# Another order of the seven products of a fast 2x2 block multiplication, and another interleaving of the steps, in a graph-network kernel

## The chip, the core and the metric

The kernel runs on one core of a Trainium2 chip. A core has five engines with a queue each: TensorE (PE in the profile; PEld is its loading of weights) multiplies matrices, VectorE (DVE), ScalarE (ACT) and GpSimd (POOL) work on elements, and SyncE (SP) issues the transfers between the main memory and the on-chip memory SBUF. TensorE writes its products into PSUM, eight banks of 128 x 512 fp32, from where VectorE and ScalarE read them. Each engine takes its instructions strictly in the order in which they were written; an instruction that waits for another engine holds up everything behind it in its own queue.

The metric is the time of one execution in microseconds (us) on the device.

## The reference

Everything is fp32. For 64 graphs of 256 nodes and 512 features, with a dense adjacency matrix each:

```
# layer 0
h = relu(adj @ (x @ W1) + b1)
h = relu(adj @ (h @ W2) + b2)
h = adj @ (h @ W3) + b3
x = layernorm(x + h)
# layer 1
q, k = split(x @ Wqk);  v = x @ Wv
agg = adj @ (k * mask)
w = (q * agg).sum(-1) * mask / sqrt(512)
x = layernorm(x + softmax(w)[:, None] * v)
```

The softmax runs over the nodes of a graph, one weight for each node.

## The kernel before

**Tiling.** Two graphs make a pair, and there are 32 pairs. A product of two matrices, cut into 2 x 2 blocks, is made with seven block products instead of eight (Strassen's scheme in Winograd's form): sums of blocks are made ahead of them (`a_sums`, `b_steps`, `t_sums`, `adj_sums`), and sums of the products behind them. This is what `seven()` (L110) writes out: `mm(n, bank, first)` issues the matmuls of product n into a PSUM bank, with `first=False` adding to what the bank holds. Three banks are used: x collects products 1, 6, 5, 3; v collects 7 and 4; y holds 2. The four blocks of the result come out as

- C11 = y + P1 (P1 copied out of x by ScalarE right after product 1, L117);
- U = P1 + P6 is copied out of x after product 6 (L126);
- after product 5 bank x holds U + P5, which ScalarE copies to `q` (L134); C22 = v + q is summed by VectorE (its adds are all in `add`, L65);
- C12 is what x holds after product 3, C21 = v + u after product 4.

With `plus`, three more blocks are added to C11, C22 and C21: GpSimd adds them to the copies of P1, q and u (`padd`, L68). For the order 1, 7, 6, 2, 5, 3, 4 this means: product 3 goes into bank x once ScalarE has copied it to q, and product 4 into bank v once VectorE has read it for C22.

`seven()` is called from three places. `support` (L306) makes x times a weight matrix, four matmuls to a product. `adj_times` (L364) makes adjacency times a matrix, two matmuls to a product; it is used in `back` (layer 0's third aggregation, with x + b3 as `plus`) and for the gather `agg`. `inner` (L543) is one of two levels of the attention: the 2 x 2 scheme is applied twice, seven outer products in the groups "a" (1, 2), "b" (6, 5), "c" (7, 4), "d" (3), each made of seven inner ones, whose order is `STEPS`, "ab" seven times, then "cd" seven times. "c" and "d" have `plus`. The weights of the inner products were summed once (`make_m`), lie in main memory, and are fetched by SP into a ring of seven tiles: each inner step issues the fetch of the tile seven steps on (`fetch`, L230). The first two aggregations (L328) use plain blocks: their four column tiles of 128 features go through ScalarE's relu (L331) into hT, in the order 2, 3, 0, 1; `lower_first` swaps the two halves, so that the sums of the next support can start with the lower half of the features. All weight matrices W1, W2, W3 are held with their rows in that swapped order.

**Stages.** Generators yield after each step: F is the front of pair i (support, aggregation, support, aggregation, support); S the sums for the next pair and x + b3; B the back of pair i-1 (the third aggregation, layer norm, transposition of the result by way of main memory, `via`); G its gather; M its attention, which ends with `results` (the two scores of each graph, L560, on VectorE, and half of v); E finishes pair i-2 (softmax with transposes on TensorE at L383 and L398, scaling of v at L601, layer norm, output). In the last round X and Y finish the two graphs of the last pair.

**What sets the order.** Three strings written out in the code, START for the first round, ORDER for rounds 1 to 31, and END for the last: each letter runs one step of that generator, and `run()` goes through the string (L631). Since every engine takes its instructions as written, these strings and the order inside the steps decide what stands behind what in all five queues.

## Time and profile before

| | |
|---|---|
| runs shown | 2795.99, 2801.28, 2804.63 us; median 2801.28 |
| the profiled execution | 2800.18 us, span 2798.4 us |
| mean granted TensorE clock | 0.994 |
| busy: TensorE, GpSimd, VectorE, ScalarE | 2741.9, 1817.1, 1718.5, 1158.0 us |
| matmul records, first and last start | 12688, 1.4 and 2788.2 us |

An fp32 matmul is recorded as two records, so a product of a support shows as 8 matmul records, one of `adj_times` as 4. The span runs from the first to the last instruction of the program; the profiled execution's own time is a little longer. A line of the timeline names start, duration, engine, line of the kernel, operation, output and inputs, shape and how many instructions were put together; in brackets is how long the engine had been idle, and who ended it. In the waits, "A <- B" means that A's engine stood idle until B was done.

The bias add x + b3 (L68, `x<-x,b3b`) takes 1.49 us on average; the additions of `plus` in `back` (`tmp<-tmp,x`) 1.41; ScalarE's copies out of a bank 0.56 (L117, L126, L134); VectorE's adds from a bank 0.62 to 0.68 (L65). A fetch into the ring lands 3.3 us after its issue in the median, the load of x, 1 MB, 6.6.

### The profile page before, as it was taken

To read this page: it belongs to the slowest core of one execution; us is meant where nothing else is said; L and a number is where in the kernel's file an instruction comes from. 1 tells how busy PE (TensorE), PEld (TensorE's weight loads), DVE (VectorE), ACT (ScalarE), POOL (GpSimd) and SP (SyncE) were. 2 spreads that over 40 slices of the span, in tenths; PEclk is the share of its full clock that TensorE was granted. 3 is DMA by queue.
4 is the path that set the end of the run, shared out by engine and by line. 5 is a ranking of instruction groups with operands and counts; after the bars stand their busy time and mean duration, and the time that the engine had idled before them with its cause. 6 is when DMAs were issued, how large, how long until landed. Compare 5 with 4: busy or idle time off the path is not lost.

```text
span 2798.4 us, 36927 instructions
## 1 busy us (share of the span) xinstructions
PE 2741.9 (98%) x12688; PEld 2370.7 (85%) x12688; DVE 1718.5 (61%) x2898; ACT 1158.0 (41%) x1888; POOL 1817.1 (65%) x1446
## 2 busy tenths in 40 slices
PE   9999999999999999999999999999999999999996
PEld 8888888888888888888888888888888888888875
DVE  4466556666556666556665566665566655666556
ACT  2334344434444334444343444344443434443444
POOL 2667766676766676666667666766666776667664
PEclk9999999999999999999999999999999999999998
DMA  6444554344554344544445543445444455434442
GB/s 216 138 125 145 160 175 133 117 141 150 160 160 135 115 145 146 174 144 129 124 144 160 175 132 112 140 146 172 150 131 125 134 160 175 132 115 145 134 153 96
DMA packets 197752, 403.45 MB, mean 144 GB/s; under 512 B 20160, under 2 KB 57408, under 8 KB 189504
## 3 DMA queue, kind: packets, MB, share of 16 engines
q1 hardware_dynamic: 197568, 401.10, 44.8%
q8 instruction: 103, 1.69, 0.3%
q14 instruction: 81, 0.66, 0.1%
HBM read 328.54 MB, written 72.48 MB: 143 GB/s over the span
## 4 chain that ended last, share of the span: by engine, by line
PE 91%; DMA 3%; POOL 2%; DVE 2%; ACT 1%; issue 1%; SPq 0%; ACTq 0%; DVEq 0%; POOLq 0%
PE ps L306 39%; PE ps L543 22%; PE ps L328 16%; PE ps L364 13%; DMA ring<-mv 3%; POOL tmp L68 2%; DVE r L65 1%; ACT tmp L134 1%; PE ps L248 1%; PE ps L383 0%; PE ps L398 0%; DMA xT<-in_xT 0%; DVE w L97 0%; POOL x L68 0%; POOL T L97 0%
## 5 line engine op out<-in xcount | busy, mean ns | idle before, releaser
L306 PE MATMUL ps<-w_T,S 128*128 128x256 f32 x2304 | 547.7, 381 | 2.4 <-POOL S L289 1.9
L306 PEld LDWEIGHTS ps<-w_T,S 128*128 128x128 f32 x2304 | 432.6, 190 | 61.4 <-POOL S L289 3.1
L65 DVE TENSOR_TENSOR R<-ps,tmp 128x512 f32<-128x512 f32 (+1 forms) x384 | 235.5, 621 | 385.5 <-PE ps L543 327.6
L328 PE MATMUL ps<-aT,sup 128*128 128x256 f32 x2048 | 457.7, 379 | 0.0
L543 PE MATMUL ps<-ring,I 128*128 128x256 f32 x1792 | 425.1, 381 | 13.8 <-DMA ring<-mv 12.1
L328 PEld LDWEIGHTS ps<-aT,sup 128*128 128x128 f32 x2048 | 389.1, 190 | 52.8
L285 POOL TENSOR_TENSOR S<-hT 128x512 f32<-128x512 f32 x64 | 81.9, 1280 | 538.1 <-ACT hT L331 538.1
L543 PEld LDWEIGHTS ps<-ring,I 128*128 128x128 f32 x1792 | 335.1, 190 | 72.6 <-ACT tmp L134 18.4
L134 ACT COPY tmp<-ps 128x512 f32<-128x512 f32 (+1 forms) x288 | 161.0, 559 | 541.9 <-PE ps L306 305.8
L65 DVE TENSOR_TENSOR sup<-ps,tmp 128x512 f32<-128x512 f32 x288 | 196.5, 682 | 244.8 <-PE ps L306 192.2
L543 PE MATMUL ps<-ring,Z 128*128 128x256 f32 x1344 | 322.6, 380 | 0.0
L68 POOL TENSOR_TENSOR tmp<-tmp,R 128x512 f32<-128x512 f32 x192 | 229.4, 1208 | 125.5 <-ACT tmp L134 50.6
L117 ACT COPY tmp<-ps 128x512 f32<-128x512 f32 (+1 forms) x288 | 161.2, 560 | 313.6 <-PE ps L306 133.6
L543 PEld LDWEIGHTS ps<-ring,Z 128*128 128x128 f32 x1344 | 256.1, 191 | 35.0
L126 ACT COPY tmp<-ps 128x512 f32<-128x512 f32 (+1 forms) x288 | 158.6, 562 | 287.9 <-PE ps L306 154.9
L306 PE MATMUL ps<-w,hT 128*128 128x256 f32 x1024 | 241.9, 379 | 0.0
L331 ACT ACTIVATE hT<-ps,b 128x512 f32<-128x512 f32 x256 | 175.6, 686 | 119.8 <-PE ps L328 114.4
L68 POOL TENSOR_TENSOR I<-Z 128x384 f32<-128x384 f32 (+1 forms) x128 | 171.8, 1363 | 77.7 <-ACT Z L521 77.0
L306 PEld LDWEIGHTS ps<-w,hT 128*128 128x128 f32 x1024 | 194.6, 190 | 26.5
L364 PE MATMUL ps<-T,aS 128*128 128x256 f32 x768 | 197.1, 386 | 2.6 <-POOL T L97 2.6
L68 POOL TENSOR_TENSOR tmp<-tmp,x 128x512 f32<-128x512 f32 x96 | 134.3, 1413 | 99.7 <-ACT tmp L134 99.7
L68 POOL TENSOR_TENSOR x<-x,b3b 128x512 f32<-128x512 f32 x128 | 189.4, 1489 | 0.0
(111 smaller groups left out, 4522.9 us busy)
## 6 DMA issues: line engine op xcount, KB each, us to landing
ring<-mv SPq DMA_DIRECT2D x672, 256.0 KB, 3.3
x<-in_xN SPq DMA_DIRECT2D x32, 1024.0 KB, 6.6
out<-v SPq DMA_DIRECT2D x64, 512.0 KB, 2.7
xT<-in_xT SPq DMA_DIRECT2D x31, 1024.0 KB, 4.8
via<-tr SPq DMA_DIRECT2D x31, 1024.0 KB, 4.3
x1T<-via SPq DMA_DIRECT2D x124, 256.0 KB, 4.4
ring<-mv SPq DMA_DIRECT2D x224, 128.0 KB, 2.7
aT<-in_adjT SPq DMA_DIRECT2D x32, 512.0 KB, 3.3
```

Of the source, the lines that this page charges most:

```text
L65: nc.vector.tensor_tensor(o, a, b, op=OP.add)
L68: nc.gpsimd.tensor_tensor(o, a, b, op=op)
L117: nc.scalar.copy(t1, x)
L126: nc.scalar.copy(u, x)
L134: nc.scalar.copy(q, x)
L248: nc.tensor.matmul(pt[:, j * P:(j + 1) * P], lhsT=wq[:, d, f * P:(f + 1) * P], rhs=wk[:, d, j * P:(j + 1) * P], start=(d == 0 and j == 0), ...
L285: eng.tensor_tensor(S[2], blk(0, 0), blk(1, 0), op=sub)
L306: nc.tensor.matmul(ps[:, g], lhsT=src[n][:, c, g], rhs=w[n][:, c], start=(first and g == 0 and c == 0), stop=(g == G - 1 and c == 1), skip ...
L328: nc.tensor.matmul(ps[:, g], lhsT=C[k][c // 2][:, g, (c % 2) * P:(c % 2 + 1) * P], rhs=aT[:, k, g], start=(g == 0 and k == 0), stop=(g == ...
L331: nc.scalar.activation(hT[c // 2][:, c % 2], ps, AF.Relu, bias=b[:, c:c + 1])
L364: nc.tensor.matmul(ps[:, g], lhsT=aS[n][:, g], rhs=mov[n][:, g], start=(first and g == 0), stop=(g == G - 1), skip_group_check=True)
L543: nc.tensor.matmul(ps[:, k], lhsT=left[n](place[o]), rhs=wt[:, k], start=(first and k == 0), stop=(k == len(outer) - 1), skip_group_check= ...
```

## The change

- In `seven()` the order is 1, 7, 6, 2, 5, 4, 3. After product 2, ScalarE copies P7 out of bank v into `t7` (with `plus`, GpSimd adds there to t7 and u). After product 5, VectorE sums C22 from bank x, which holds U + P5, and t7. Product 4 then goes into bank v, and C21 = v + u; product 3 goes last into bank x, and C12 is what it then holds. ScalarE makes as many copies as before. `INNER`, the order in which the ring's weights are stored and fetched, follows.
- The column tiles of the aggregations go in the order 0, 1, 2, 3; `blocks` replaces `lower_first`, and only the input xT and W1 keep the lower half first.
- `results(1)` comes before `results(0)`, and X and Y change places.
- In the last round r lies where xT did, and the transposed x1T is in two tiles, each with its own copies out of PSUM.
- All strings of steps are different. The last full round has a string of its own (the same as ORDER), and whatever it leaves of the attention of pair 30 would be run in END as "N"; the padding that follows a string is named for each round.

```diff
--- before.py
+++ after.py
@@ -111,6 +111,7 @@
 
 
 
+
         x = bank(shape)
         mm(1, x, True)
         t1 = shaped(shape)
@@ -127,28 +128,25 @@
         yield
         y = bank(shape)
         mm(2, y, True)
+        t7 = shaped(shape)
+        nc.scalar.copy(t7, v)
+        if plus is not None:
+            padd(t7, t7, plus[2])
+            padd(u, u, plus[1])
         c11(y, t1)
         yield
         mm(5, x, False)
-        q = shaped(shape)
-        nc.scalar.copy(q, x)
-        if plus is not None:
-            padd(q, q, plus[2])
-        else:
-            c22(v, q)
-        yield
-        mm(3, x, False)
-        if plus is not None:
-            c22(v, q)
-            padd(u, u, plus[1])
-        c12(x)
+        c22(x, t7)
         yield
         mm(4, v, False)
         c21(v, u)
         yield
-
-
-    def load_w(w, n):
+        mm(3, x, False)
+        c12(x)
+        yield
+
+
+    def load_w(w, n, lower=False):
 
 
         q = [tmp().rearrange("p (c f) -> p c f", c=2) if b == 1 else
@@ -156,7 +154,7 @@
         ts = [const.tile([P, 2, HD], FP, name=f"w{n}_{s}") for s in KEYS]
 
         def load(b):
-            k, j = 1 - b // 2, b % 2
+            k, j = (1 - b // 2 if lower else b // 2), b % 2
             nc.sync.dma_start(q[b], w[k * HD:(k + 1) * HD, j * HD:(j + 1) * HD].rearrange("(c p) f -> p c f", p=P))
 
         def begin():
@@ -180,7 +178,7 @@
 
     warm(10)
     wl = {}
-    begin, end = load_w(W1, 1)
+    begin, end = load_w(W1, 1, True)
     xTs = load_xT(0, begin)
     for _ in end():
         pass
@@ -211,7 +209,7 @@
 
 
     OUTER = ((1, 2), (6, 5), (7, 4), (3,))
-    INNER = (1, 7, 6, 2, 5, 3, 4)
+    INNER = (1, 7, 6, 2, 5, 4, 3)
     STEPS = "ab" * 7 + "cd" * 7
     place = {n: k for k, n in enumerate(n for q in OUTER for n in q)}
     w_dram = [dram.tile([P, 7, len(q), HD], FP, name=f"mv_{k}", bufs=1) for k, q in enumerate(OUTER)]
@@ -292,9 +290,9 @@
             eng.tensor_tensor(S[3], blk(0, 1), S[1], op=sub)
         return {1: blk(0, 0), 2: blk(0, 1), 4: blk(1, 1), 5: S[0], 6: S[1], 7: S[2], 3: S[3]}, first, rest, last
 
-    def lower_first(hT):
-
-        return lambda h, k: hT[1 - k][:, :, :, h * P:(h + 1) * P]
+    def blocks(hT, lower=False):
+
+        return lambda h, k: hT[1 - k if lower else k][:, :, :, h * P:(h + 1) * P]
 
     def support(src, w, last=None):
 
@@ -320,8 +318,8 @@
 
 
         hT = [pool.tile([P, 2, G, N], FP, name="hT", tag="act", bufs=2) for _ in range(2)]
-        src, first, rest, last = a_sums(lower_first(hT))
-        for c in (2, 3, 0, 1):
+        src, first, rest, last = a_sums(blocks(hT))
+        for c in range(DC):
             ps = bank()
             for g in range(G):
                 for k in range(NH):
@@ -329,9 +327,9 @@
                                      rhs=aT[:, k, g], start=(g == 0 and k == 0), stop=(g == G - 1 and k == NH - 1),
                                      skip_group_check=True)
             nc.scalar.activation(hT[c // 2][:, c % 2], ps, AF.Relu, bias=b[:, c:c + 1])
+            if c == 1:
+                first()
             if c == 3:
-                first()
-            if c == 1:
                 rest()
             yield
         return src, last
@@ -415,7 +413,7 @@
 
         fs = [lambda: None] * 3
         if i + 1 < NPAIR:
-            put["S"], *fs = a_sums(lower_first(put["xT"]))
+            put["S"], *fs = a_sums(blocks(put["xT"], True))
         for f in fs:
             f()
             yield
@@ -428,7 +426,7 @@
 
     def back(i, C, aS, x, end, put):
         Ts = t_sums(C)
-        r = pool.tile([P, G, NH, D], FP, name="r", bufs=1)
+        r = pool.tile([P, G, NH, D], FP, name="r", tag="xT" if end else "r", bufs=1)
         xb = lambda h, j: x[:, :, h, j * HD:(j + 1) * HD]
         rb = lambda h, j: r[:, :, h, j * HD:(j + 1) * HD]
         st = small.tile([P, NH, G, 6], FP, name="st")
@@ -463,8 +461,8 @@
         xmb = [[xm[:, :, h, j * HD:(j + 1) * HD] for j in range(2)] for h in range(2)]
         if end:
             warm(20)
-            x1T = pool.tile([P, 2, 2, G, N], FP, name="x1T", bufs=1)
-            x1b = lambda h, k: x1T[:, k, :, :, h * P:(h + 1) * P]
+            x1T = [pool.tile([P, 2, G, N], FP, name="x1T", tag="act", bufs=2) for _ in range(2)]
+            x1b = lambda h, k: x1T[k][:, :, :, h * P:(h + 1) * P]
             for h, g in hg:
                 apply(h, g)
             yield
@@ -474,7 +472,8 @@
                 pt = bank((P, 2, 2, P))
                 for c in range(DC):
                     nc.tensor.transpose(pt[:, c // 2, c % 2], r[:, g, h, c * P:(c + 1) * P], ident)
-                (nc.scalar.copy if h else nc.vector.tensor_copy)(x1T[:, :, :, g, h * P:(h + 1) * P], pt)
+                for k in range(2):
+                    (nc.scalar.copy if h else nc.vector.tensor_copy)(x1T[k][:, :, g, h * P:(h + 1) * P], pt[:, k])
         else:
             tr = pool.tile([P, 4, 32, NH, 2, 2, G], FP, name="tr", tag="gt", bufs=1)
             x1T = pool.tile([P, P, NH, 2, 2, G], FP, name="x1T", bufs=1)
@@ -584,10 +583,10 @@
                 C = pool.tile([P, 2, G, 2, HD], FP, name="R", tag="Za", bufs=1)
                 run.update(c=inner(2, C, B), d=inner(3, B[:, :1], B[:, :1]))
             if n == 26:
-                yield from results(0)
+                yield from results(1)
             next(run[k])
             yield
-        yield from results(1)
+        yield from results(0)
 
     def finish(i, prev, gs=range(G)):
 
@@ -621,29 +620,31 @@
 
 
 
-    ORDER = ("FBFEFFEFEBBBBFBBFBFBFBFFBBBFEFBEBGFSGFFGEGFEEGEEFEFFFEMMGGMFMMFMMMMMSMSMMMMMMMMMMFMS"
-             "MMFMMMMMFMMSESMSMSMFMSMSMMMFFSM")
-    START = ("BFFBBFFFBFBBBBFBBFBBBBBBBFBFBBFFBBBBBBBFFBFBBBFBFBBFBBFBBBFFBFBBBBFBBFFBFBBBBBFSBBBB"
-             "SSSBBFSSBSFSBSBSBBBSBSB")
-    END = ("BEEBEEBEEBBBBEBBBBEBEEBBBGGEMMBBMGGMEMGMMGMBMMMGMMMMMMMMMMMMMMMMMMMMMMMMXMMMMMXXMMYX"
-           "XMMMXMYMMMYYXXYXYXXMYYYXYYY")
-
-    def run(order, **gens):
+    ORDER = ("BFEFFFEBFBEFBBBFBBFBBFFFBFBESBEFBBGFFGEFEEGEGFFEFESFFGMMGSFEMGMMFMMMMMMMMMMMMMMMMMFM"
+             "MMMMMSFMMMSSMMSMSSFMFSMFMMEMSMMFM")
+    START = ("FBBFBFFFBBFBBBFBBFBBBBFBFFBBBBBBFBBFBBBBBBBBFFFFBBFBBBBBBFFBBSBFFBFBBSFBBBFFSBBBFSBB"
+             "BBSBFBSBFBSSSSBSBBBSBBB")
+    LAST = ("BFEFFFEBFBEFBBBFBBFBBFFFBFBESBEFBBGFFGEFEEGEGFFEFESFFGMMGSFEMGMMFMMMMMMMMMMMMMMMMMFM"
+            "MMMMMSFMMMSSMMSMSSFMFSMFMMEMSMMFM")
+    END = ("EEBEBEBEEBBBEEEBBBEEBBBBBBGMGMGBGMMBMEMMMMMGGMMMBMMMMGMMMMMMMMMMMMMMMMMMXMXMMMMXMMYM"
+           "XMXXMXMYMYYYXXYYMMXXMYXYYYY")
+
+    def run(order, rest, **gens):
         res = {}
-        for k in order + "FSBGMEXY" * 90:
+        for k in order + rest * 90:
             if k in gens and k not in res:
                 try:
                     next(gens[k])
                 except StopIteration as e:
                     res[k] = e.value
-        assert len(res) == len(gens)
+        assert all(k in res for k in rest if k in gens)
         return res
 
     def later(put, f):
         yield from f(put)
 
     state = prev = None
-    xS, *fs = a_sums(lower_first(xTs))
+    xS, *fs = a_sums(blocks(xTs, True))
     for f in fs:
         f()
     for i in range(NPAIR + 1):
@@ -658,13 +659,17 @@
             for k in "GM":
                 gens[k] = later(done, lambda d, k=k: d[k])
         if prev is not None:
-            gens["E"] = finish(i - 2, prev)
-        if i == NPAIR:
-            for g, k in enumerate("XY"):
+            gens["E"] = later(prev, lambda d, i=i: finish(i - 2, d[0]))
+        if i < NPAIR - 1:
+            res = run(ORDER if i else START, "FSBGME", **gens)
+        elif i < NPAIR:
+            res = run(LAST, "FSBGE", **gens)
+            rest = gens["M"]
+        else:
+            for g, k in enumerate("YX"):
                 gens[k] = later(done, lambda d, g=g: finish(NPAIR - 1, d[g], [g]))
-        order = START if i == 0 else ORDER if i < NPAIR else END
-        res = run(order.replace(" ", ""), **gens)
-        prev = done.get(1)
+            run(END, "NBGMEXY", N=rest, **gens)
+        prev = done if i else None
         if i < NPAIR:
             state = (res["F"], put["aS"], put["x"])
             xTs, xS = put.get("xT"), put.get("S")
```

## The prediction

> **What bounds the kernel now.** I read the page first: busy time of the engines, the slices, the chain that ended last.
>
> ```profile
> span 2798.4 us, 36927 instructions
> PE 2741.9 (98%) x12688; PEld 2370.7 (85%) x12688; DVE 1718.5 (61%) x2898; ACT 1158.0 (41%) x1888; POOL 1817.1 (65%) x1446
> PE   9999999999999999999999999999999999999996
> PE ps L306 39%; PE ps L543 22%; PE ps L328 16%; PE ps L364 13%; DMA ring<-mv 3%; POOL tmp L68 2%; DVE r L65 1%; ACT tmp L134 1%; PE ps L248 1%; PE ps L383 0%; PE ps L398 0%; DMA xT<-in_xT 0%; DVE w L97 0%; POOL x L68 0%; POOL T L97 0%
> ```
>
> TensorE is the bound: 98% busy, 91% of the chain. The number of matmuls does not change, so the change can only win the holes between them, or open new ones. I measured the holes as distances between the starts of successive matmul records, against the 0.2157 us that undisturbed ones keep (8 records in 1.73 us below, which is one product of a support; a product of `back` is 4 records, 0.863 us). All holes together are 81 us of the span. Next the waits, longest first, of which these bear on the change:
>
> ```profile
> POOL tmp L68 <- ACT tmp L134: 150.3, 95, 5.9
> DVE r L65 <- POOL tmp L68: 24.4, 32, 2.1
> PEld ps L364 <- DVE r L65: 18.6, 32, 1.3
> PE ps L543 <- DMA ring<-mv: 12.1, 14, 1.6
> ```
>
> (Who waited for whom: us in total, times, longest.) Only the last two rows are TensorE's. 32 times it waits at L364, once per pair; 14 times for a weight tile of the ring. Third, TensorE's timeline around L364 in one middle pair:
>
> ```profile
> 1025.85 1.03 PE L364 MATMUL ps<-sup,aT 128*128 128x256 f32 x4
> 1026.74 1.13 PE L364 MATMUL ps<-T,aS 128*128 128x256 f32 x4
> 1027.71 1.89 PE L306 MATMUL ps<-w,S 128*128 128x256 f32 x8
> 1029.43 1.03 PE L364 MATMUL ps<-sup,aS 128*128 128x256 f32 x4
> 1030.61 1.13 PE L364 MATMUL ps<-T,aT 128*128 128x256 f32 x4 [0.15 <-DVE r L65]
> 1031.58 1.89 PE L306 MATMUL ps<-w_T,xT 128*128 128x256 f32 x8
> ```
>
> The reader should subtract starts: product 3 of `back` (sup,aS) takes 1.18 us to the next start instead of 0.863, product 4 (T,aT) 0.97. Steady pairs without a ring hole repeat every 84.59 to 84.60 us, of which 0.86 us is holes; 0.20 of these stand at the softmax transposes, the rest in the lines shown.
>
> **The change, part by part.**
>
> *Order of the products in `back`.* Removed is the chain product 5, ACT copy L134, POOL add L68, DVE add into r, product 4: (1.18 - 0.863) + (0.97 - 0.863) = 0.42 us. Removed too is the edge of product 5 (T,aS at 1026.74, after 6): 0.89 + 0.97 - 2 x 0.863 = 0.135 us, since ACT has one copy less to make between 6 and 3. Together 0.557 us in each of 31 pairs: 17.3 us. Product 4 now finds its bank v free, because P7 was copied out two products earlier. The new wait is product 3 on the DVE add that reads bank x. Product 4 (2 matmuls) and a product of a support (4) lie between, 2.6 us; from the end of a product to DVE's start the timeline shows about 0.25 us, the add L65 is 0.68. Queued ahead of it on DVE are four softmax scalings (L601, 4.40 us in this pair), two adds of the next support, a bn_stats and the add for C11; walked through in the new order, they leave the bank's release some 1.6 us early. With every scaling at its largest in the trace, 1.76 us, it would be 1.0 late, 31 us over the run; at their mean, 1.16, it is not late, and I take nothing. Behind that add wait this pair's bn_stats and, through product 3, its layer norm. The two POOL adds (L68, 1.41 us each) and the ACT copy (0.56) move one or two steps ahead in their queues; the 150.3 us that POOL spent waiting for ACT show that POOL had room there.
>
> *Order in the supports and the attention.* In the steady pairs product 3 after an ACT copy cost next to nothing there (other work stood between), so nothing is won. Lost may be two narrow places that I found by counting matmuls (0.4313 us each) in the new order of instructions. (i) Support 3: product 3 stands 7 matmuls, 3.0 us, behind product 5, and waits for a DVE add that is queued behind two scores (L560), the add for C11 (0.68) and half of v (0.67 to 1.14). (ii) The softmax transposes (L383 before, L381 after) come 11 matmuls, 4.75 us, after product 3 of "d", where 19 stood before; between lie DVE adds of 0.69 and 0.41 and two scores. What a score costs is the question:
>
> ```profile
> 1008.63 0.75 DVE L560 SCALAR_TENSOR_TENSOR gt<-R,mask_s,gt 128x512 f32<-128x512 f32 x1
> 1009.31 1.74 DVE L560 SCALAR_TENSOR_TENSOR gt<-R,mask_s,gt 128x512 f32<-128x512 f32 x1
> 1013.69 1.40 DVE L560 SCALAR_TENSOR_TENSOR gt<-R,mask_s,gt 128x512 f32<-128x512 f32 x1
> 1015.02 1.20 DVE L560 SCALAR_TENSOR_TENSOR gt<-R,mask_s,gt 128x512 f32<-128x512 f32 x1
> ```
>
> (Start, us, on VectorE.) The same instruction takes 0.75 us alone and 1.74 beside POOL's `x + b3b`. With two of 1.20 to 1.27, the median and mean, DVE is some 0.5 us early at (i) and 0.2 to 1.0 early at (ii). With two of 1.74 it is about 0.6 late at (i) and, at worst, 1.1 late at (ii): 1.7 us per pair, 51 us over 30 pairs. The other end is nothing, as these places are not waited at before. I take 0.2 us per pair, 6 us: near the lower end, because the four scores above average 1.27. [...]
>
> *The ring.* Its holes average 0.52 us per pair, 15 us in 29 pairs. They fall at the third fetch of an a/b phase, issued on SP's queue just behind the 1 MB load of x (6.6 us to land), 13 matmuls before use. Load, fetches and distance stand the same after; I keep the 15 us (ends: 0, and 1.7 us in every pair, 49). In the c/d phase the fetches now stand 13 to 15 matmuls (5.6 us at least) ahead of use instead of 17 to 19; in one pair of the trace they landed 2.4 to 4.1 us after issue, so I count nothing (upper end, landing like the 6.6 us of x: 1 us per pair, 30). Other SP work (`via`, x1T, out, aT) keeps its place to within a few matmuls; xT is fetched 12 matmuls earlier into a quiet stretch.
>
> *Columns in order 0..3, upper rows first.* First sums wait for two activations as before; distances are the same to a matmul. Nothing; the POOL sums S have 538 us of waiting in front of them as cover.
>
> *Start.* Three supports run back to back there:
>
> ```profile
> 52.96 1.97 PE L306 MATMUL ps<-w,S 128*128 128x256 f32 x8 [0.77 <-ACT tmp L134]
> 73.25 1.97 PE L306 MATMUL ps<-w,S 128*128 128x256 f32 x8 [0.77 <-ACT tmp L134]
> 77.29 3.28 PE L306 MATMUL ps<-w_T,hT 128*128 128x256 f32 x8 [2.08 <-DVE sup L65]
> ```
>
> Each loses about 1.0 us at product 3 (0.92 ahead of it by starts, 0.09 after; the first at 18.05). Product 4's 1.73 us now stands where that hole was, and covers 0.25 + 0.68 of DVE. That wins 3 us. The 2.08 at 77.29 is DVE busy with the sums of the attention's weights and stays, at product 3. Bounds: 0 (the holes move to that queue) and -6 (that wait goes too).
>
> *End.* The last `back` stands alone:
>
> ```profile
> 2734.91 1.13 PE L364 MATMUL ps<-sup,aS 128*128 128x256 f32 x4 [0.73 <-ACT tmp L134]
> 2736.97 1.13 PE L364 MATMUL ps<-T,aT 128*128 128x256 f32 x4 [0.94 <-DVE r L65]
> ```
>
> Both waits go, 1.67 us; about 0.5 comes back at product 3 (0.25 + 0.68 + rest against 0.863), and x1T in two tiles makes 8 copies of half the size from 4, on two engines, some +0.3. With the earlier sums T, the sum is -1.5 (bounds -5, +2: X and Y change places, and each wait in the tail is 2 to 4 us).
>
> **Sum.** The profiled execution took 2800.18 us (span 2798.4), 1.1 under the median of the runs, 2801.28. 2800.2 - 17.3 + 6 - 3 - 1.5 = 2784.4, about 2784.
>
> **Rivals.**
>
> *R1, slower: VectorE late for bank x and for the softmax.* Mechanism (i) and (ii) at the long scores: 2800.2 - 17.3 - 4.5 + 51 = 2829. It decides from 0.557 us per pair on, plus 0.15 for start and end: a second score at 1.74 instead of 1.2 nearly does it at (i). For it: 1.74 is in the trace, and POOL is busy with x + b3b and aS just then. Against: the mean is 1.27, the largest of 128 is 1.77, and a delay at (i) also delays what (ii) stands behind.
>
> *R2, no change: the same places take 0.3 to 0.6 us per pair.* 2800.2 - 21.8 + 9 to 18 = 2787 to 2796; only its upper half is within 0.3%.
>
> *R3, slower: ring fetches.* With 1.73 us less distance, c/d fetches that land late cost up to 1 us per pair: 2778 + 30 = 2808, with a few us of (i) 2815. For it: a third fetch already lands late in 14 pairs. Against: these stand behind x's load, those do not.
>
> *R4, faster still: no new hole.* 2800.2 - 21.8 = 2778. *R5, nothing is won:* were the holes merely taken over by the ring, steady pairs would stay at 2796 or so. Against: where a ring hole occurs, the 0.42 at L364 is there as well, and x's load is released by TensorE's own progress.
>
> **How the numbers follow.** Chances: the forecast 0.45 (own range 2776 to 2792), R4 0.22, R2 and R5 0.17, R1 0.10, R3 0.06. 0.3%, 8.4 us, is about what a measurement of this kernel can tell from no change: faster is under 2793, slower over 2810. R1's lower half and part of R2 fall between: faster 0.69, same 0.17, slower 0.14. For 8 in 10 the range goes from 2774 (R4 with a better start) to 2808 (R3, R1 just past its turn); the far part of R1 is left out.
>
> **What would show it.** Right: pairs without a ring hole repeat every 84.0 to 84.2 us; no row of PEld L362 waiting for DVE r; the pair's starts at L362 0.86 apart; no 0.77 waits at L304 near 50 and 70 us. Wrong: rows of TensorE at L304 waiting for DVE sup, at L381 waiting for DVE gt in most of 32 pairs, at L362 for DVE r; ring waits well over 12 us; DVE's L559 mean far over 1.27.

## The result, and the profile after

The changed kernel takes 2779.19 us (median of 4 runs, 2775.05 to 2780.69); the kernel before, in the same comparison, 2800.02 us. The ratio is 0.9923, with a 95% interval of 0.9904 to 0.9942: 0.8% faster, 4.8 us below the forecast of 2784 and inside its own range. In a second comparison, with more runs, the same two kernels stood at 2790.21 and 2802.65 us, ratio 0.9946 (0.9930 to 0.9962). Why the gain is 21 us in the one and 12 in the other is answered below: it is not the change that differs.

The page of the changed kernel, its span, busy times and chain by line:

```profile
span 2778.9 us, 37024 instructions
PE 2731.4 (98%) x12688; PEld 2377.9 (86%) x12688; DVE 1723.4 (62%) x2900; ACT 1143.7 (41%) x1890; POOL 1795.9 (65%) x1446
PE ps L304 41%; PE ps L542 22%; PE ps L326 16%; PE ps L362 14%; DMA ring<-mv 3%; PE ps L246 1%; DVE v L600 0%; DVE gt L559 0%; PE ps L381 0%; PE ps L396 0%; DMA xT<-in_xT 0%; DVE R L65 0%; POOL S L286 0%; POOL tmp L68 0%; DVE st L607 0%
```

The line numbers have moved by two or so: L304 are the supports (306 before), L362 `adj_times` (364), L542 the attention, L326 the aggregations, L381 the first softmax transposes. The 2% of POOL tmp L68 in the chain is 0% now, and DVE r L65 and ACT tmp L134, 1% each, are no longer named. The same in the waits (us in total, times, longest):

```profile
POOL tmp L68 <- ACT tmp L132: 147.4, 63, 4.4
PE ps L542 <- DMA ring<-mv: 13.1, 13, 1.5
PE ps L381 <- DVE gt L559: 7.7, 3, 3.5
PEld ps L362 <- DVE r L65: 1.8, 1, 1.8
```

PEld waited 32 times for DVE r; one time is left, in the last round. The ring's wait stands as it did. TensorE's timeline around `back` in one pair:

```profile
1022.69 1.03 PE L362 MATMUL ps<-sup,aT 128*128 128x256 f32 x4
1023.55 1.03 PE L362 MATMUL ps<-T,aS 128*128 128x256 f32 x4
1024.41 1.03 PE L362 MATMUL ps<-T,aT 128*128 128x256 f32 x4
1025.28 1.89 PE L304 MATMUL ps<-w,S 128*128 128x256 f32 x8
1027.00 1.03 PE L362 MATMUL ps<-sup,aS 128*128 128x256 f32 x4
1027.87 4.48 PE L326 MATMUL ps<-aT,sup 128*128 128x256 f32 x20
```

Every product of `back` now takes 0.86 to 0.87 us to the next start; in the kernel before it was 0.89, 0.97, 1.18 and 0.97. Product 4 (T,aT) follows product 5 at once, and product 3 (sup,aS) comes last, with a support's product between.

I add up TensorE's holes as in the prediction: the distance between the starts of two successive records, less 0.2157 us, wherever it is over 0.225. The start reaches to the first product with the next pair's xT, the end begins after the last product of a support.

| holes, us | before | after |
|---|---|---|
| start | 10.4 | 7.0 |
| rounds 1 to 31 | 44.7 | 29.4 |
| of these: at the attention's matmuls, nearly all the ring's | 20.2 | 16.9 |
| `back`, product 4 | 13.1 | 0 |
| `back`, product 5 | 4.1 | 0 |
| edges at the softmax transposes | 6.0 | 6.0 |
| support 3, product 3 | 0 | 6.5 |
| all else | 1.2 | 0 |
| end | 25.8 | 24.8 |
| together | 80.9 | 61.2 |

Pairs in which the ring is not late repeat every 84.15 us instead of 84.59. The 0.44 us are 0.56 of `back` less 0.21 at support 3, and 0.10 in the attention, where the old order lost as much to the copy at its inner product 3 (in the kernel before it shows only where the ring is not late; in run 12, where it never is, in all 31 rounds).

The difference, 19.7 us, is close to the 19.5 between the two profiled executions, 2800.18 and 2780.69. The row that is new, 6.5 us at support 3's product 3, is seen where VectorE frees bank x. VectorE in a middle pair:

```profile
1001.48 1.73 DVE L559 SCALAR_TENSOR_TENSOR gt<-R,mask_s,gt 128x512 f32<-128x512 f32 x1
1003.14 1.74 DVE L559 SCALAR_TENSOR_TENSOR gt<-R,mask_s,gt 128x512 f32<-128x512 f32 x1
1004.81 0.68 DVE L65 TENSOR_TENSOR sup<-ps,tmp 128x512 f32<-128x512 f32 x1
1005.42 1.14 DVE L65 TENSOR_TENSOR v<-R 128x512 f32<-128x512 f32 x1
1006.48 0.68 DVE L65 TENSOR_TENSOR sup<-ps,tmp 128x512 f32<-128x512 f32 x1
```

and TensorE at the same time:

```profile
1006.74 0.59 PE L542 MATMUL ps<-ring,I 128*128 128x256 f32 x2
1007.31 1.96 PE L304 MATMUL ps<-w,S 128*128 128x256 f32 x8
1009.11 1.03 PE L362 MATMUL ps<-sup,aT 128*128 128x256 f32 x4
```

C22 is the last of VectorE's lines: it starts at 1006.48 and ends after 1007.1. Product 3 could start at 1006.74 + 0.43 = 1007.17 and starts at 1007.31: 0.14 us, and 0.07 more on its first records. Both scores in front take their full 1.73 and 1.74 us.

In the start, product 3 no longer waits for a copy; two waits of about 2 us are left, the second of them at a product 3, but for VectorE:

```profile
12.44 1.99 PE L304 MATMUL ps<-w_T,S 128*128 128x256 f32 x8 [2.06 <-POOL S L287]
53.38 1.89 PE L304 MATMUL ps<-w,S 128*128 128x256 f32 x8
74.81 1.97 PE L304 MATMUL ps<-w,S 128*128 128x256 f32 x8 [1.65 <-DVE sup L65]
```

### The profile page after: what moved, and what is told of

Same layout as the page of the kernel before. It is cut to its first block, busy times and chain, and to the rows that moved or that the text cites. A ratio compares the mean times of both kernels' runs of the same rounds, so it can differ in the third digit from the quotient of the medians.

```text
span 2778.9 us, 37024 instructions
## 1 busy us (share of the span) xinstructions
PE 2731.4 (98%) x12688; PEld 2377.9 (86%) x12688; DVE 1723.4 (62%) x2900; ACT 1143.7 (41%) x1890; POOL 1795.9 (65%) x1446
## 4 chain that ended last, share of the span: by engine, by line
PE 93%; DMA 3%; DVE 2%; issue 1%; POOL 1%; ACT 0%; SPq 0%; POOLq 0%; ACTq 0%; DVEq 0%
PE ps L304 41%; PE ps L542 22%; PE ps L326 16%; PE ps L362 14%; DMA ring<-mv 3%; PE ps L246 1%; DVE v L600 0%; DVE gt L559 0%; PE ps L381 0%; PE ps L396 0%; DMA xT<-in_xT 0%; DVE R L65 0%; POOL S L286 0%; POOL tmp L68 0%; DVE st L607 0%
## 5 line engine op out<-in xcount | busy, mean ns | idle before, releaser
L304 PE MATMUL ps<-w_T,S 128*128 128x256 f32 x2304 | 539.7, 379 | 3.8 <-POOL S L287 2.8
L304 PEld LDWEIGHTS ps<-w_T,S 128*128 128x128 f32 x2304 | 435.1, 190 | 63.9 <-POOL S L287 4.0
L326 PE MATMUL ps<-aT,sup 128*128 128x256 f32 x2048 | 457.7, 379 | 0.0
L65 DVE TENSOR_TENSOR R<-ps,tmp 128x512 f32<-128x512 f32 (+1 forms) x384 | 230.5, 622 | 365.5 <-PE ps L542 350.3
L542 PE MATMUL ps<-ring,I 128*128 128x256 f32 x1792 | 428.5, 381 | 13.3 <-DMA ring<-mv 13.1
L326 PEld LDWEIGHTS ps<-aT,sup 128*128 128x128 f32 x2048 | 389.0, 190 | 52.8
L542 PEld LDWEIGHTS ps<-ring,I 128*128 128x128 f32 x1792 | 339.7, 190 | 64.7 <-issue 15.1
L127 ACT COPY tmp<-ps 128x512 f32<-128x512 f32 (+1 forms) x288 | 158.0, 560 | 446.7 <-PE ps L542 183.8
L65 DVE TENSOR_TENSOR sup<-ps,tmp 128x512 f32<-128x512 f32 x288 | 197.4, 686 | 211.6 <-PE ps L304 211.6
L542 PE MATMUL ps<-ring,Z 128*128 128x256 f32 x1344 | 321.6, 379 | 0.0
L68 POOL TENSOR_TENSOR tmp<-tmp,R 128x512 f32<-128x512 f32 (+1 forms) x192 | 213.1, 1137 | 160.2 <-DVE R L579 141.2
L542 PEld LDWEIGHTS ps<-ring,Z 128*128 128x128 f32 x1344 | 255.4, 190 | 34.7
L307 ACT COPY sup<-ps 128x512 f32<-128x512 f32 x96 | 56.2, 585 | 457.1 <-PE ps L304 303.6
L68 POOL TENSOR_TENSOR I<-Z 128x384 f32<-128x384 f32 (+1 forms) x128 | 177.7, 1409 | 100.6 <-DVE Z L523 97.1
L304 PE MATMUL ps<-w,hT 128*128 128x256 f32 x1024 | 241.9, 379 | 0.0
L118 ACT COPY tmp<-ps 128x512 f32<-128x512 f32 (+1 forms) x288 | 158.8, 563 | 172.1 <-PE ps L304 86.0
L304 PEld LDWEIGHTS ps<-w,hT 128*128 128x128 f32 x1024 | 194.6, 190 | 26.4
L68 POOL TENSOR_TENSOR tmp<-tmp,x 128x512 f32<-128x512 f32 x96 | 120.5, 1270 | 128.7 <-ACT tmp L132 128.4
L65 DVE TENSOR_TENSOR gt<-ps,tmp 128x512 f32<-128x512 f32 x96 | 65.4, 682 | 222.6 <-PE ps L362 222.6
L68 POOL TENSOR_TENSOR x<-x,b3b 128x512 f32<-128x512 f32 x128 | 202.3, 1600 | 0.0
```

Of the source, the lines that this page charges most:

```text
L65: nc.vector.tensor_tensor(o, a, b, op=OP.add)
L68: nc.gpsimd.tensor_tensor(o, a, b, op=op)
L118: nc.scalar.copy(t1, x)
L127: nc.scalar.copy(u, x)
L304: nc.tensor.matmul(ps[:, g], lhsT=src[n][:, c, g], rhs=w[n][:, c], start=(first and g == 0 and c == 0), stop=(g == G - 1 and c == 1), skip ...
L307: steps = seven(mm, (P, G, HD), lambda y, t: add(C[0][0], y, t), lambda x: nc.scalar.copy(C[0][1], x), lambda v, t: add(C[1][0], v, t), la ...
```

## The experiments

My theory was the prediction's: the order of the products takes the chain through ScalarE's copy out of `back` and the start, at the price of a place where VectorE is late; columns and pattern of steps are nothing by themselves. Its rivals: the pattern of steps carries the gain; the ring does. Times of a run are compared with the kernel before on the same chip (given as "before"), holes with the table above.

**1. The new order alone, in the old kernel.**

```diff
 # before.py, seven(): the body of the changed kernel
-    INNER = (1, 7, 6, 2, 5, 3, 4)
+    INNER = (1, 7, 6, 2, 5, 4, 3)
-                yield from results(0)
+                yield from results(1)
...
-        yield from results(1)
+        yield from results(0)
...
-            for g, k in enumerate("XY"):
+            for g, k in enumerate("YX"):
...
-        prev = done.get(1)
+        prev = done.get(0)
```

> The kernel before with the new order of the seven products, and only what that forces (results(1) before results(0), X and Y changed over); steps, columns and weights as before. Theory (the order of the products wins the holes of back): the waits of PEld L361 for DVE r go, 17 us. But product 3 is last now, and the aggregation that follows starts with column tile 2, which needs C12, ScalarE's copy of product 3: 1 matmul (0.43 us) between where the copy takes 0.25 + 0.56 + 0.05. By the holes that the kernel before shows for the same distance (0.92 + 0.09 us at product 3 in the start), two aggregations per pair lose 1.0 us each, 62 us: 2800 - 17 + 62 - 1 = about 2844, with waits of TensorE at L325 for ACT sup near 60 us. Rival (the column order is worth nothing, as the prediction costs it, and the order of the products is all there is): about 2783. Rival (the new pattern of steps wins it): about 2800, with L361 still waiting for DVE r.

Measured: 2913.64 us (before 2795.24), ratio 1.0419 (1.0404 to 1.0435). The holes of product 4 in `back` are gone, and 123.2 us stand at L325, the aggregations, 4.0 per pair. TensorE in one pair (the two aggregations of a pair):

```profile
1009.32 1.89 PE L303 MATMUL ps<-w,S 128*128 128x256 f32 x8
1013.16 5.45 PE L325 MATMUL ps<-aT,sup 128*128 128x256 f32 x24 [1.94 <-ACT sup L306]
...
1072.83 1.89 PE L303 MATMUL ps<-w,S 128*128 128x256 f32 x8
1075.44 7.17 PE L325 MATMUL ps<-aT,sup 128*128 128x256 f32 x32 [0.72 <-ACT sup L306]
```

and ScalarE ahead of the first of them:

```profile
1010.41 2.22 ACT L614 ACTIVATE v<-v,nb,rs 128x512 f32<-128x512 f32 x3 [0.44 <-DVE nb L372]
1012.54 0.56 ACT L306 COPY sup<-ps 128x512 f32<-128x512 f32 x1
```

The second aggregation loses what was expected, 2.61 - 1.73 = 0.88 us and 0.10 behind it. The first loses 3.84 - 1.73 = 2.11, since the copy of C12 is queued behind three layer-norm activations of E; and behind 15 of the 30 waits of this kind the records that follow come up to 0.21 us further apart, 1.7 us in all, 0.85 per pair on average (see the last section). The mechanism holds and its size was doubled. The rival that the columns are worth nothing is out.

**2. The order and the columns, old pattern of steps.** As 1, and:

```diff
-        for c in (2, 3, 0, 1):
+        for c in range(DC):
...
-            if c == 3:
+            if c == 1:
                 first()
-            if c == 1:
+            if c == 3:
                 rest()
 # and blocks() for lower_first(), W2 and W3 loaded upper rows first
```

> As the run before this one, with the column tiles of the aggregations in the order 0..3 and the weights' rows to go with it; the pattern of steps is still the one of before. Theory: the 62 us are not there, as column tiles 0 and 1 need C11 and C21, which are 8 matmuls and more behind; the 13.1 us of product 4 in back and the 3 us of the start are won, the 4.2 us edge at product 5 of back stays (3 matmuls behind the copy of U, as before), and support 3's product 3 finds DVE early (two scores ahead, but no v): 2800 - 13 - 3 = 2784, range 2778 to 2790. Rival (the pattern of steps carries the gain): 2795 or more.

Measured: 2787.44 us (before 2795.24), ratio 0.9973 (0.9962 to 0.9984): the 123 us are gone with the columns, but the gain is only 7.8 us, not the 16 that were expected, though the time lies inside the expected range. By the trace, product 4 of `back` has won its 13.1. The edge at product 5 is still there (4.5), support 3's product 3 has a hole of 9.6 (0.31 per pair, more than in the changed kernel), and the start is as long as before, 10.9 of holes: the waits at product 3 of 0.77 have gone, and others have grown, and behind two of them the records come at half the rate. Its timeline:

```profile
12.12 3.59 PE L303 MATMUL ps<-w_T,S 128*128 128x256 f32 x8 [2.07 <-POOL S L286]
...
77.36 3.57 PE L303 MATMUL ps<-w,S 128*128 128x256 f32 x8 [3.17 <-DVE sup L65]
```

The second was 2.08 before and is 1.65 in the changed kernel. Leaving the attention's holes out (10.1 here), the holes are 60.6 before, 54.1 with order and columns, 44.2 in the changed kernel: 6.5 us come with the order and its columns, 9.9 with the pattern of steps and the rest. Of these holes, about 1.7, 3.3 and 0 us are records at half rate in the start, which follow some of the waits there and not others (last section); without them it is 8 and 7. The rival is right about half of the gain, roughly. The new pattern with the old order throughout wasn't tried.

**3. The old order in `back` alone.** In the changed kernel:

```diff
-        yield from seven(mm, (P, G, HD), c11, c12, c21, c22, plus=plus)
+        yield from (seven if plus is None else seven_old)(mm, (P, G, HD), c11, c12, c21, c22, plus=plus)
```

> The changed kernel with the old order 5, 3, 4 and the copy q in back alone. Theory: product 3 stands 1 matmul behind product 5 there (0.9 + 0.1 us, the copy), product 4 waits for copy, POOL add and DVE add as before, 7 matmuls behind product 5 and mostly covered by the first hole: 1.0 to 1.4 us per pair, 31 to 43 us, 2810 to 2822, with L400 waiting for ACT tmp and DVE r again. Rival (what is won is won in the start, the end and the ring, and back is hidden): under 2787.

Measured: 2808.07 us (before 2795.24), ratio 1.0046 (1.0025 to 1.0066); 29.2 us of holes at product 3, nothing at product 4:

```profile
1030.51 1.03 PE L400 MATMUL ps<-T,aS 128*128 128x256 f32 x4
1032.21 1.13 PE L400 MATMUL ps<-sup,aS 128*128 128x256 f32 x4 [0.68 <-ACT tmp L131]
```

1.70 - 0.86 = 0.84, and 0.10 behind it: 0.94 per pair, a little under the 1.0 to 1.4 expected, since product 4 does not wait as it was expected to. So the gain in `back` is real, but within the new pattern the old order would cost 29.2 us, against the 17.2 that it cost in its own pattern, which kept a support's product between 5 and 3. Order and pattern belong together.

**4. The old order in the supports alone.**

```diff
-        steps = seven(mm, (P, G, HD), lambda y, t: add(C[0][0], y, t), ...
+        steps = seven_old(mm, (P, G, HD), lambda y, t: add(C[0][0], y, t), ...
```

> The changed kernel with the old order 5, 3, 4 in the supports alone. Theory: in the start product 3 waits for ScalarE again, 3 x 1.0 us; in the pairs C21 is now the last block, summed by DVE (0.25 + 0.68 + 0.05 us at least), 2 matmuls before the aggregation that starts with it, some 0.2 to 0.6 us in each of one or two aggregations per pair; the 0.21 us hole at product 3 of support 3 moves to product 4 or goes. Together 2779 + 3 + 6 to 35 = 2788 to 2817. Rival (the supports gain nothing from the order, it is back alone): 2776 to 2784.

Measured: 2844.34 us (before 2795.24), ratio 1.0165 (1.0143 to 1.0187). The start has 9.7 us of holes instead of 7.0, as expected; the aggregations have 57.4, more than the 6 to 35 that I allowed. TensorE:

```profile
1050.21 0.59 PE L364 MATMUL ps<-aT,sup 128*128 128x256 f32 x2
1051.78 6.74 PE L364 MATMUL ps<-aT,sup 128*128 128x256 f32 x30 [0.97 <-DVE sup L65]
...
1073.89 0.59 PE L364 MATMUL ps<-aT,sup 128*128 128x256 f32 x2
1074.84 5.01 PE L364 MATMUL ps<-aT,sup 128*128 128x256 f32 x22 [0.35 <-DVE sup L65]
```

Both aggregations of a pair stop after one matmul for C21: 1.57 - 0.43 = 1.14 and 0.95 - 0.43 = 0.52 us, with an edge of 0.1 each. The hole at support 3's product 3 was expected to move or go, but 6.9 us stay there; product 3 waits for ScalarE's copy again. Columns 0..3 need product 4 early, as columns 2, 3, 0, 1 needed product 3 early: column order and product order are one decision.

**5. Half of v one step later.** In ORDER and LAST, two letters change places, so that VectorE does C22 of support 3 ahead of `add(v...)`; TensorE's order is the same:

```diff
-             "MMMMMSFMMMSSMMSMSSFMFSMFMMEMSMMFM")
+             "MMMMMSFMMMSSMMSMSSFFMSMFMMEMSMMFM")
```

> The changed kernel with one letter of the pattern moved in all rounds: the step with half of v (VectorE, 0.67 to 1.14 us) comes behind the step of support 3's product 5 and its C22, instead of ahead of it. TensorE's order is the same. Theory (product 3 of support 3 is late by 0.21 us per pair because DVE reaches C22 late, behind two scores and v): C22 comes 0.6 to 1.1 us earlier, the holes at L304 w,S of 6.5 us go, 2779 - 6.5 = 2773. Rival (the hole comes from elsewhere: the POOL sum S or the weights): no change in these holes, 2779.

Measured: 2782.74 us (before 2795.49), ratio 0.9957 (0.9945 to 0.9970); no gain over the changed kernel in the trace. The holes at product 3 are gone (6.5 to 0), but 9.1 us stand at the first softmax transposes, 0.21 in each pair and 2.8 in the end, where 1.9 stood, all of it in the end. VectorE and then TensorE:

```profile
1003.96 1.77 DVE L65 TENSOR_TENSOR v<-R 128x512 f32<-128x512 f32 x1
1008.29 1.20 DVE L559 SCALAR_TENSOR_TENSOR gt<-R,mask_s,gt 128x512 f32<-128x512 f32 x1
```

```profile
1007.72 1.89 PE L304 MATMUL ps<-w,xT 128*128 128x256 f32 x8
1009.65 0.38 PE L381 MATMUL ps<-ident,w 128*2 128x128 f32 x2
```

The add into v took 1.77 us instead of 1.14, the last score ended near 1009.5, and the transposes, due at 1009.45, came at 1009.65. The cause of the first hole is shown; what I had not seen is that both narrow places share one stretch of VectorE, and that moving this work within it only moved the hole.

**6. The same add done twice.**

```diff
-            add(v[:, g, 1], flat(C[:, 0])[:, g], flat(C[:, 1])[:, g])
+            for _ in range(2 if g else 1):
+                add(v[:, g, 1], flat(C[:, 0])[:, g], flat(C[:, 1])[:, g])
```

> The changed kernel with that add into v done twice, so that DVE is 0.67 to 1.14 us later at C22 of support 3 in each pair. Theory: DVE is already late there, so every us counts: 31 x 0.7 to 1.1 = 21 to 35 us more, 2800 to 2814, all of it at L304 w,S. Rival (slack is left there, the prediction's 0.5 us): 6 to 16 us more at most, 2785 to 2795.

Measured: 2838.38 us (before 2795.49), ratio 1.0149 (1.0131 to 1.0167). The holes at product 3 grow from 6.5 to 58.3 us, by 1.67 per pair. VectorE, then TensorE:

```profile
1023.72 2.82 DVE L65 TENSOR_TENSOR v<-R 128x512 f32<-128x512 f32 x2
```

```profile
1025.05 0.59 PE L542 MATMUL ps<-ring,I 128*128 128x256 f32 x2
1027.29 1.97 PE L304 MATMUL ps<-w,S 128*128 128x256 f32 x8 [1.64 <-DVE sup L65]
```

Two adds take 2.82 us, 1.68 more than the one of 1.14 above: TensorE pays it in full there. The price of 0.67 to 1.14 was too low. The likely reason is POOL: in the changed kernel its three x + b3b stand there from 1002.62 to 1007.69, and the one add ends at 1006.56, so that a second one would meet them too.

**7. The load of x in four parts.**

```diff
-        nc.sync.dma_start(t, xN[i].rearrange("p (g h f) -> p g h f", g=G, h=NH))
+        src = xN[i].rearrange("p (g h f) -> p g h f", g=G, h=NH)
+        parts = [lambda g=g, h=h: nc.sync.dma_start(t[:, g, h], src[:, g, h]) for g in range(G) for h in range(NH)]
+        # pair 0: all at once; else todo.extend(parts)
...
                 fetch(at[0] + RING)
+                if at[0] % len(uses) in (8, 10, 12, 13) and todo:
+                    todo.pop(0)()
```

> The changed kernel with the 1 MB load of x cut in four parts of 256 KB, issued behind the ring fetches of attention steps 8, 10, 12 and 13 instead of in one piece just ahead of the third fetch. Theory (the ring holes come from the load of x standing ahead of the fetches in the queue): the waits for DMA ring<-mv fall from 13.1 us to under 3, 2779 - 14 to 17 = 2763 to 2766. Rival (the fetches are late because all 16 DMA engines are loaded then, x or not): holes within 5 us of before. Rival (x comes late for POOL's x + b3b): POOL waits for DMA x, and holes at L362 for DVE r or at L304.

Measured: 2771.84 us (before 2795.49), ratio 0.9916 (0.9903 to 0.9930), its runs within 1 us of each other. The third fetch is no longer late, its mean time to spare going from 0.43 to 2.18 us; but 12.6 us of ring holes now stand at the fetches for steps 20 and 21, whose time to spare fell from 2.1 and 2.3 us to 0.26 and 0.19. Half right: the load of x makes the hole, and here too it moved to where it was put.

**8. Both, 5 and 7.**

> Both edits, the add into v behind C22 and x in four parts. If the two holes are independent: 2779 - 6.5 - 15 = about 2757, steady pairs 83.9 to 84.0 us apart throughout. If the load of x only happened to absorb other lateness, less than the sum of the two.

Measured: 2772.05 us (before 2795.49), ratio 0.9920 (0.9907 to 0.9932): no more than 7 alone. With x in parts, the holes at product 3 were down to 2.4 us by themselves (POOL does x + b3b earlier by up to 0.8 us and more, and the first score takes 0.81 to 1.74 us instead of 1.73), and moving v puts 3.1 us into the pairs at the first softmax transposes.

**9. The changed kernel again**, beside 10 and 11.

> The changed kernel unchanged, beside the next two on the same chip, and for a second profile of it. Theory: the ring's holes, 9 to 24 us over the kernels run so far with the same load of x, vary from execution to execution, and the 3.3 us less of them in the first profile is chance: steady holes without the ring's stay 14.3 us (6.5 of them at L304 w,S), the ring's lie anywhere between 9 and 24. Rival (the new order helps the ring): 16 to 18 us again.

Measured: 2790.21 us, 2781.91 to 2795.94 over 12 runs (before 2802.65, 2795.57 to 2816.97 over 17). The profile has the same 6.5 us at product 3, and the same 12.5 in rounds 1 to 31 without the ring (the 14.3 expected counts the first wait of the end, 1.9, too); the ring's holes are 29.8 us instead of 16.9. This is all of the difference between the two profiled executions, 2780.69 and 2792.89. So one kernel's ring holes differ by 13 us between two executions, which is outside even the range that I had set, and the 3.3 us less of the first comparison say nothing about the change.

**10. Both halves of v behind the last score.**

```diff
-            add(v[:, g, 1], flat(C[:, 0])[:, g], flat(C[:, 1])[:, g])
-            put[g] = r, v, w
+            for k in (g,) if i == NPAIR - 1 else (1, 0) if g == 0 else ():
+                add(v[:, k, 1], flat(C[:, 0])[:, k], flat(C[:, 1])[:, k])
+                put[k] = r, v, w
```

> The changed kernel with both halves of the add into v behind the last score, in all rounds but the last; TensorE's order is the same. Theory (VectorE's whole stretch from the first score to the softmax is what is too long, so that moving v within it only moved the hole): DVE does C22 of support 3 at least 1.1 us earlier and the last score 0.6 to 1.1 us earlier; both the 6.5 us at L304 w,S and the 7 to 9 us that appeared at L381 when v was moved by one step are gone: 6.5 us less than the changed kernel. Rival (the scores run faster or slower with what POOL does beside them, and take back what is won): less than 3 us.

Measured: 2785.01 us (the changed kernel on the same chip 2790.21, before 2802.65), ratio to before 0.9931 (0.9910 to 0.9953). Both holes are gone, at product 3 (6.5 to 0) and at L381 (1.9 to 1.0): undisturbed pairs repeat every 83.94 us, where the changed kernel needs 84.15 and the kernel before 84.59. The medians differ by 5.2 us; the intervals overlap, so it is the trace that shows these 6.5 us.

**11. 10, and x in four parts behind other steps.**

```diff
-                if at[0] % len(uses) in (8, 10, 12, 13) and todo:
+                if at[0] % len(uses) in (8, 13, 15, 17) and todo:
```

> As the run before, and the load of x in four parts of 256 KB behind the ring fetches of attention steps 8, 13, 15 and 17, whose next fetches have 2.3 us or more to spare in the changed kernel; the first try put them behind 8, 10, 12 and 13 and moved the holes to the fetches for steps 20 and 21 (12 us). Theory: ring holes under 3 us, 6.5 + 14 = 20 us less than the changed kernel, steady pairs all at 83.94 us. Rival (the DMA engines are full in this stretch, wherever x is put): ring holes of 8 us or more again.

Measured: 2759.54 us (before 2802.65), 2757.38 to 2760.16 over 5 runs, ratio 0.9838 (0.9816 to 0.9861). It beats both kernels; the changed one by 30.7 us and not by 20, since the ring cost that one 29.8 in its profile beside this run and not the 14 that were reckoned with. Its page:

```profile
span 2755.6 us, 37054 instructions
PE 2720.1 (99%) x12688; PEld 2380.5 (86%) x12688; DVE 1699.0 (62%) x2900; ACT 1144.3 (42%) x1890; POOL 1801.9 (65%) x1446
```

In rounds 1 to 31 it has 6.0 us of holes, the edges at the softmax transposes; the ring's are 0.06, in one pair. In the 25 pairs 3 to 27 no fetch had less than 0.44 us to spare, outside them one had 0.15. No wait for DMA ring<-mv is left. In the changed kernel's second profile they were:

```profile
PE ps L542 <- DMA ring<-mv: 23.4, 23, 1.9
```

**12. The same four parts in the kernel before.** The edit of 11 to the load of x, and nothing else.

> The kernel before, with nothing but the load of x in four parts of 256 KB behind the ring fetches of attention steps 8, 13, 15 and 17. Theory (the ring's holes have nothing to do with the change, and were there to be had without it): the waits for DMA ring<-mv go from 12.1 us to under 2, the kernel becomes faster by its ring holes, 15 to 20 us, and its executions agree more closely than those of before. Rival (the parts collide with the fetches of the c/d phase in the old pattern, or x comes late for POOL's x + b3b): less than 8 us.

Measured: 2783.36 us, four runs within 0.6 us of each other (before 2814.00, 2801.41 to 2815.90), ratio 0.9898 (0.9870 to 0.9925). No wait for DMA ring<-mv is left. Against the first profile of before, holes in rounds 1 to 31 fall from 44.7 to 28.2 us; against the runs beside it the gain is 31 us. That the ring cost more in those is the likely reason; their traces were not taken. These 16 to 31 us were to be had without any of the change, and are as much as the change itself brought.

## Why the prediction was right, and where not

**`back`, 17.3 us.** Measured 13.1 + 4.1 = 17.2. But the reason given for the second term was wrong. ScalarE has no copy less to make between 6 and 3 (u and t7 now, u and q before), and with the new order in the old pattern (run 2) the edge at product 5 stays, 4.5 us. It goes because the new pattern puts a support's product between products 6 and 5, so that the copy of U has 7 matmuls of cover instead of 3; in run 3, with the old order in the new pattern, it is gone too.

**The two narrow places, 6 us.** Measured 6.5 at (i), nothing at (ii). The sum came out by luck of two errors. I took the scores at 1.20 to 1.27 us, their median and mean; at (i) they take 1.73 and 1.74, because each of them meets a GpSimd addition with some 1.2 us still to run, in 31 of the 32 pairs. A mean over the run is no price for one place. At 1.74 I had counted 0.6 late, and it is 0.21 with its edge. At (ii) the scores take 1.11 and 1.20, and the transposes are on time. R1's mechanism is real, as runs 5 and 6 show: it decides from 0.557 us per pair on, and stayed at 0.21.

**The scores beside POOL.** I read the rows as 0.75 us alone and 1.74 beside x + b3b. That was wrong: the score of 0.75 ran beside GpSimd too. Of the 128 scores in each kernel's profile, 125 (before) and 124 (after) begin while a GpSimd addition runs, and every one of them ends 0.55 us behind the end of that addition (0.545 to 0.554); the few others take 0.74 us. So the price of a score in these two profiles is what is left of the addition that it meets, plus 0.55. The first score in the lines above, 1001.48 to 1003.21, meets this one, which ends at 1002.66:

```profile
1001.39 1.27 POOL L290 TENSOR_TENSOR S<-hT,S 128x512 f32<-128x512 f32 x1
```

That is 0.74 - 0.55 = 0.19 us less than if the whole score came behind the addition. By these rows (an estimate) an addition of 1.26 that is met at its start makes the score 1.26 + 0.55 = 1.81 us; the longest of the 128 scores of the changed kernel took 1.75.

**The attention, nothing won.** The steady pairs had 0.86 us of holes, of which I had placed 0.20 and 0.557. The other 0.10 was the copy at the attention's inner product 3, where I had put next to nothing; the new order takes it away, up to 3.0 us over the run (run 12).

**Columns 0..3, nothing.** Right as a term of this sum, and wrong as a thing to call nothing. The cover that I should have named is product 4, which comes ahead of product 3: without the new column order, the new product order loses 123 us (run 1), and with the new columns the old order in the supports loses 57 (run 4). I looked at the distances of the sums S, and not at which block of the support the first column tile reads.

**Start, -3 us.** Measured -3.3. The mechanism is there: three holes at product 3, of 0.96, 1.01 and 1.01 us, are gone (the 0.77 waits are gone in run 2, too, and come back in run 4). That the rest nearly cancels is luck. The waits for POOL S at 12 us and for the weights at 8 us grew by 0.56 and 0.49 us, one of 0.36 was added, the wait for DVE sup went from 2.08 to 1.65, and 1.2 us of records at half rate behind it are not there. In run 2 the three holes are gone as well, and nothing is won: the wait for DVE sup grew to 3.17, and 1.7 us of records at half rate were added. What makes the wait for DVE sup shorter in the changed kernel was not tested.

**End, -1.5 us.** Measured -1.0: the waits of the last `back` for its copy and for DVE r fell less than expected, from 1.67 to 1.39 us (at product 3). Two waits for POOL T, 0.78 and 1.83 us, are gone, and the two at the first softmax of the tail grew from 0.65 and 2.30 to 1.74 and 3.23.

**The ring, kept at 15 us.** The distances are the same, as said, and the holes were 20.2 and 16.9 (by the waits 12.1 and 13.1; the 20.2 hold some 1.5 of the copy at inner product 3, in the pairs without a ring hole). That the term can be held constant was the mistake: 16.9 and 29.8 in two executions of one kernel. This accounts for most of the 4.8 us by which the result passed the forecast in one comparison, and puts it 6 us on the other side (2790) in the next. The c/d fetches, nearer to their use by 1.73 us, were not late in the 25 pairs of the first profile that I looked at: those for steps 18 to 27 had 0.61 us to spare at the least, with the old distance 2.3. R3 did not happen, but not by much.

So the time was right, and most of its terms. What it attributed to the order of products is a gain of three parts together: in the old kernel the order alone costs 118 us, order and columns win 8, and with the pattern the gain is 12 to 21.

## What to carry to other kernels

When the order of partial results is changed, ask first which of them the next stage reads first; here that was worth 123 us. Price an instruction by the row of its own place, not by the mean of its kind, and when two waits hang on one engine's stretch, take work out of the stretch rather than move it inside (runs 5 and 10). And before tuning the order of compute, look at the variable term: a 1 MB load in front of small fetches cost 17 to 30 us here, differently from run to run, and four parts between fetches with time to spare removed it in both kernels.

## What the runs showed of the hardware

**TensorE's rate after a wait.** In run 2, after a wait of 2.07 us, eight records took 3.59 us instead of 1.99: they come about 0.42 us apart instead of 0.22. In the changed kernel the same place, after 2.06 us, shows full rate. The granted clock in the profile (PEclk) shows why: it is 0.50 for 3.41 us in run 2, and 1.00 in the changed kernel. Run 2 first, then the changed kernel:

```profile
core 0: us, PE busy (x) PEld busy (x) DVE busy (x) ACT busy (x) POOL busy (x), PEclk, DMA share, GB/s
10.05:12.12 2.07, 0.00 (x2) 0.00 (x1) 0.90 (x2) 0.00 (x0) 1.93 (x2) 1.00 1.09 346
12.35:15.76 3.41, 3.41 (x9) 2.70 (x9) 1.99 (x3) 0.01 (x1) 1.05 (x1) 0.50 1.10 352
15.77:22.50 6.73, 6.73 (x32) 5.93 (x32) 3.46 (x6) 1.05 (x2) 0.00 (x0) 1.00 1.04 383
...
12.44:14.20 1.76, 1.76 (x8) 1.58 (x9) 0.70 (x2) 0.00 (x0) 1.26 (x1) 1.00 1.10 349
```

The kernel before has it at 77.29: after a wait of 2.08 us eight records take 3.28 us, and the recorded clock is 0.50 from 77.84 to 81.25, again 3.41 us. After the wait of 1.65 us ahead of 74.81 in the changed kernel it stays at 1.00. In the profiles of before and of the changed kernel (the first one) the recorded clock changes only at whole multiples of 3.4133 us from its first change, to within 0.03 us; that first change stands at 6.16 us in the one and at 4.70 in the other. The wait before, 75.21 to 77.29, lies whole between two such points, 74.43 and 77.84; the one in the changed kernel that full rate follows, 10.38 to 12.44, has such a point inside, 11.53. In run 2 the wait, 10.05 to 12.12, lies whole in the 3.41 us ahead of 12.35, where the half clock begins. Run 1 has 30 such waits, of 1.94 or 1.95 us, 15 of them followed by half the clock; its mean granted clock is 0.986, where it is 0.994 before. So in these runs a wait of 2 us cost its own length, and up to 1.7 us more where half the clock followed. What decides whether it follows is not shown.

**Transfers.** How late a fetch behind a 1 MB load lands varies between executions of one program: the third fetch of a phase landed 4.7 us after its issue in the first profile of the changed kernel and 5.6 in the second (medians of 29 pairs), and 2.7 with x in four parts (run 11). The times follow: the runs of the kernel before spread over 21 us in one comparison, those of the four kernels with x in four parts over 0.6 to 3.9 us. Why the landing varies is not shown.
